# A decoder's cross attentions: heads weighed two chunks at a time, five PSUM banks for scores, queries from unpadded weights

## The chip, the cores and the metric

The kernel runs on one core of a Trainium2 chip. The metric is the device time of one execution in microseconds (us); lower is better. The chip's engines each run their own queue in order: TensorE (PE; its weight loads are listed as PEld), VectorE (DVE), ScalarE (ACT), GpSimd (POOL) and SyncE (SP, which issues DMAs).

## The reference, cut to what matters

The reference is a decoder of four layers over x (8 batches, 112 tokens, 256 features), each layer with a self attention, a cross attention to a context of 8 x 375 x 128, and an FFN. Three of the four cross attentions (layers 1, 2 and 3) go through one helper. With the layer norm in front, layer 1's is

```python
qh = (q @ Wq + bq).reshape(B, LQ, HEADS, D_K).transpose(0, 2, 1, 3)
kh = (k @ Wk + bk).reshape(B, LKV, HEADS, D_K).transpose(0, 2, 1, 3)
vh = (v @ Wv + bv).reshape(B, LKV, HEADS, D_K).transpose(0, 2, 1, 3)
attn = jax.nn.softmax(jnp.einsum('bhqd,bhkd->bhqk', qh, kh) * scale, axis=-1)
out = jnp.einsum('bhqk,bhkd->bhqd', attn, vh)
return concat @ Wo + bo
```

There are 16 heads. Layers 1 and 3 have 16 features a head (the code calls this case `dense`), layer 2 has 32. Layer 3 has no biases.

## The kernel before, in words

`cross` (L1260 to L1447) is that helper; `l1_xattn`, `a2_attend` and `l3_xattn` call it. It takes one batch of 112 tokens after the other, and the 16 heads of a batch in four **chunks** c of four heads j. One chunk of one batch is a **step**; there are 32 in each of the three attentions. What a step consists of:

- `score` (L1326): four matmuls, one a head, each on its own 32 rows of the array, into four PSUM banks `sc` of 112 x 375. TensorE runs an fp32 matmul as two instructions, so the trace has eight.
- `exponent` (L1333): for each head a DVE maximum over the scores (L1338) and an ACT exponential (L1342; in layer 2 L1344, which also sums) into `xe`.
- `turn` (L1347): three transposes of a head's `xe` into a bank `tr`, of which there are two in turn, and the copy `xeT` out of it: by DVE for heads 0 and 2 (L1359), by ACT for heads 1 and 3 (L1357).
- `attend` (L1362): the values times the exponentials, 12 matmuls (24 instructions) on 32 columns of the array each, into one quarter of the bank `av`. After the fourth chunk ACT copies the whole bank to `xoT` (L1377).

Beside these there is work for the neighbouring batches: `key` (L1291, evacuated by ACT) and `value` (L1301, evacuated by DVE) for the next batch; `summed` (L1379: eight tiny matmuls that gather the softmax's denominators, a DVE reciprocal, a POOL copy), `divide` (L1391: four transposes into a `tr` bank, a DVE product) and `result` (L1402: the output projection and the sum into x) for the batch before; and `query` (L1313) for the second half of the tokens. Keys, values, queries, denominators and results all use the one bank `mm`.

The eight PSUM banks are thus: `mm` 1, `av` 1, `tr` 2, `sc` 4.

In layers 1 and 3 a head has 16 features, but a row tile of the array has 32. Keys are kept packed, two heads in 32 rows (`nk` = 2 chunks of 128 rows). `_halves` (L81) therefore spreads the query weights over 512 columns, with zeros where the other head of a pair lies, so that a score over 32 rows sees one head. A half's queries are then four products of 128 columns instead of two.

The order is written out by hand (L1414 to L1447, `manual_schedule` for PE, DVE and ACT): each of these engines executes its instructions in the order of the calls. For a step that is: turn 0, turn 1, key (or summed or divide), turn 2, the scores of the next step, turn 3, the maxima and exponentials of the next step, value, query, result, attend. What lies outside of that block is placed among it by the framework's scheduler.

Of the kernel before, what the change touches and what calls it, by code (L numbers as in the profile page):

```python
# [46 lines left out]
def _fm(w):  # L47

    k, n = w.shape
    return w.reshape(k // P, P, n).transpose(1, 0, 2).reshape(P, -1)  # L50


def _col(v):

    return v.reshape(-1, P).T
# [22 lines left out]
    return w.reshape(-1, 16, 16)[:, _SLOTS].reshape(w.shape)  # L78


def _halves(w):  # L81

    out = np.zeros((w.shape[0], 4, 4, 2, 16), w.dtype)
    a = w.reshape(-1, 16, 16)[:, _SLOTS].reshape(-1, 4, 4, 16)
    for n in range(4):
        out[:, n, :, n % 2] = a[:, n]
    return out.reshape(-1, 512)

_SHIFT = np.tile(np.arange(32) == 16, 16).astype(np.float32)
# [33 lines left out]
def _weights(inp):  # L125
    def g(layer):
# [46 lines left out]
            ("l1a_bo", _row(a("bo"))),  # L173
        ],
        [
            ("l1x_wq", _fm(_halves(xa("Wq")))),
            ("l1x_wk", xa("Wk")),
            ("l1x_wv", _slots(xa("Wv"))),
            ("l1x_bv", _row(_slots(xa("bv")[None])[0])),
# [10 lines left out]
    for j in range(2):  # L190
# [1 line left out]
    v1 = [  # L192
        ("l1a_bq", _col(_spread(a("bq")[None])[0])),
        ("l1a_bk", _col(_spread(a("bk")[None])[0] + _SHIFT)),
        ("l1x_bq", _col(_halves(xa("bq")[None])[0])),
        ("l1x_bk", _col(xa("bk"))),
    ]

# [40 lines left out]
    for pf in ("a1", "a2"):  # L239
        for n in ("lnx_g", "lnx_b", "lny_g", "lny_b", "ln3_g", "ln3_b", "li2_b"):  # L240
# [10 lines left out]
    ]  # L251
    last = [
        [
            ("l3x_wq", _fm(_halves(xa("Wq").T))),
            ("l3x_wk", wkv[:, :D]),
            ("l3x_wv", _slots(wkv[:, D:])),
        ],
# [6 lines left out]
        ("l3f_s_in", np.broadcast_to(f("s_in")[None, :], (P, 1))),  # L264
        ("l3f_s_in_down", np.broadcast_to(f("s_in_down")[None, :], (P, 1))),
    ]
    return (blobs, ternary, last), own, ints, raw, v0 + v1 + v2 + v3


# [110 lines left out]
class _Kernel:  # L380
# [879 lines left out]
    def cross(self, name, cT, qsrc, wq, wk, wv, wo, hd, scale, finish, ctx, bq=None, bk=None, bv=None):  # L1260
# [16 lines left out]
        work = ctx.enter_context(tc.tile_pool(name=f"{name}_w", bufs=2))  # L1277
        ps1 = ctx.enter_context(tc.tile_pool(name=f"ps1_{name}", bufs=1, space=PSUM))
        ps = ctx.enter_context(tc.tile_pool(name=f"ps_{name}", bufs=2, space=PSUM))
        ps4 = ctx.enter_context(tc.tile_pool(name=f"ps4_{name}", bufs=4, space=PSUM))  # L1280

        values = [self.t(acts, [P, NCH, 16, 32], f"xv{i}") for i in range(2)]
        dense = hd == 16
# [7 lines left out]
        def key(b, c):  # L1291
            if c == 0:
                keys[b] = self.t(work, [P, nk, CTX], "xkT")
            pm = self.t(ps1, [P, 512], "mm")[:, :CTX]
            self.mm(pm, [(wk[:, c * P : (c + 1) * P], cT[:, b * CTX : (b + 1) * CTX])])
            if bk is None:
                nc.scalar.copy(keys[b][:, c, :], pm)
            else:
                nc.scalar.activation(keys[b][:, c, :], pm, AF.Identity, bias=self.v(bk, c))

        def value(b, i):  # L1301
            pm = self.t(ps1, [P, 512], "mm")[:CH, : 16 * hd]
            at = b * CTX + i * CH
            self.mm(pm, [(cT[:, at : at + CH], wv)])
            src, dst = pm.rearrange("p (h d) -> p h d", h=16), values[b % 2][:CH, i, :, :hd]
            if bv is None:
                (nc.vector.tensor_copy if b else nc.scalar.copy)(dst, src)
            else:
                nc.vector.tensor_tensor(dst, src, bv[:CH].rearrange("p (h d) -> p h d", h=16), ALU.add)
# [15 lines left out]

        def score(b, c):  # L1326
            toks = slice(b * S, (b + 1) * S)
            es[b, c] = [self.t(ps4, [P, 512], "sc")[:S, :CTX] for _ in range(4)]
# [4 lines left out]
        def exponent(b, c):  # L1333
            if c == 0 and not dense:
                sums[b] = self.t(self.small, [P, 16], "xsu")[:S]
            for j, sc in enumerate(es[b, c]):
                nm = self.t(self.small, [P, 1], f"xnm{j}")[:S]
                nc.vector.tensor_reduce(nm, sc, AX.X, ALU.max, negate=True)  # L1338
                e = self.t(work, [P, CTX], f"xe{j}")[:S]
                at = 4 * c + j  # L1340
                if dense:
                    nc.scalar.activation(e, sc, AF.Exp, bias=nm)  # L1342
                else:
                    nc.scalar.activation(e, sc, AF.Exp, bias=nm, accum_out=sums[b][:, at : at + 1])  # L1344
                es[b, c][j] = e

        def turn(b, c, j):  # L1347
            tp = self.t(ps, [P, 512], "tr")
            e = es[b, c][j]
            for i in range(NCH):  # L1350
                nc.tensor.transpose(  # L1351
                    tp[:CH, i * S : (i + 1) * S], e[:, i * CH : (i + 1) * CH], self.ident[:S, :S]
                )
            eT = self.t(work, [P, NCH, S], f"xeT{j}")[:CH]
            src = tp[:CH, : NCH * S].rearrange("p (c s) -> p c s", c=NCH)
            if j % 2:
                nc.scalar.copy(eT, src)  # L1357
            else:
                nc.vector.tensor_copy(eT, src)  # L1359
            eTs[b, c, j] = eT  # L1360

        def attend(b, c):  # L1362
            if c == 0:
                avs[b] = self.t(ps1, [P, 512], "av")
            for i in range(NCH):
                for j in range(4):
                    nc.tensor.matmul(  # L1367
                        avs[b][32 * j : 32 * j + 32, c * S : (c + 1) * S],
                        values[b % 2][:CH, i, 4 * c + j, :],
                        eTs[b, c, j][:, i, :],  # L1370
                        start=i == 0,
                        stop=i == NCH - 1,
                        skip_group_check=True,
                    )
            if c == 3:
# [15 lines left out]
        def divide(b):  # L1391
            tp = self.t(ps, [P, 512], "tr")
            for c in range(4):
                nc.tensor.transpose(
                    tp[:, c * S : (c + 1) * S],
                    sums[b][:, 4 * c : 4 * c + 4, :].rearrange("p h d -> p (h d)"),
                    self.ident[:S, :S],
                )
            oT = oTs[b]
            nc.vector.tensor_tensor(oT, tp[:, : 4 * S].rearrange("p (c s) -> p c s", c=4), oT, ALU.mult)  # L1400

        def result(b):  # L1402
            finish(b, self.project(ps1, b, [oTs[b][:, c, :] for c in range(4)], wo))
# [3 lines left out]
        for i in range(NCH):  # L1407
            value(0, i)
        qsrc(ps, 0)
        for c in range(4):  # L1410
            query(0, c)
        qsrc(ps, 1)
        steps = [(b, c) for b in range(NB) for c in range(4)]
        with tc.manual_schedule(engines={ET.PE, ET.DVE, ET.Activation}):  # L1414
            score(0, 0)
            exponent(0, 0)
            for n, (b, c) in enumerate(steps):
                turn(b, c, 0)
                turn(b, c, 1)

                if not dense or c % 2 == 0:
                    if b + 1 < NB:
                        key(b + 1, c * nk // 4)
                elif b > 0:
                    (summed, divide)[c // 2](b - 1)
                turn(b, c, 2)
                if n + 1 < len(steps):
                    score(*steps[n + 1])
                turn(b, c, 3)
                if n + 1 < len(steps):  # L1430
                    exponent(*steps[n + 1])
                if c < 3 and b + 1 < NB:
                    value(b + 1, c)
                if c == 3 and b < 2:
                    query(1, 2 * b)
                    query(1, 2 * b + 1)
                if not dense and b > 0 and c == 1:
                    divide(b - 1)
                if b > 0 and c == 3:
                    result(b - 1)  # L1440
                attend(b, c)
# [1237 lines left out]
```

## Time and profile before

| | us |
|---|---|
| median of three runs | 2160.9 (2160.12 to 2161.86) |
| the profiled execution, its own time | 2162.92 |
| span of that execution, first to last instruction | 2161.1 |
| PE busy in the span | 1930.8 (89%) |
| DVE busy | 1388.4 (64%) |
| ACT busy | 867.8 (40%) |
| mean granted TensorE clock | 0.948 |
| transposes of layer 1's cross attention, first and last start | 727.6 and 889.7 |
| the same in layer 2 | 1389.1 and 1556.8 |
| the same in layer 3 | 1880.8 and 2041.4 |

Times in the trace count from the span's start. A line of the timeline gives start, duration, engine, line of the kernel, operation, output and inputs by the program's names, shape, how many instructions were merged into the line, and in brackets how long the engine was idle before it and who released it. A merged line's duration runs to the end of its last instruction; matmuls are pipelined, so the next group starts before that. The three attentions take some 490 us of the span together.

### The profile page before, as it was taken

To read this page: it belongs to the slowest core of one execution; us is meant where nothing else is said; L and a number is where in the kernel's file an instruction comes from. 1 tells how busy PE (TensorE), PEld (TensorE's weight loads), DVE (VectorE), ACT (ScalarE), POOL (GpSimd) and SP (SyncE) were. 2 spreads that over 40 slices of the span, in tenths; PEclk is the share of its full clock that TensorE was granted. 3 is DMA by queue.
4 is the path that set the end of the run, shared out by engine and by line. 5 is a ranking of instruction groups with operands and counts; after the bars stand their busy time and mean duration, and the time that the engine had idled before them with its cause. 6 is when DMAs were issued, how large, how long until landed. Compare 5 with 4: busy or idle time off the path is not lost. (4 is left out here: it accounts for less than half of the span.)

```text
span 2161.1 us, 45441 instructions
## 1 busy us (share of the span) xinstructions
PE 1930.8 (89%) x17912; PEld 1242.8 (58%) x17912; DVE 1388.4 (64%) x3907; ACT 867.8 (40%) x2420; POOL 279.0 (13%) x480
## 2 busy tenths in 40 slices
PE   7999999898898899889899989899999997899844
PEld 3555544465666566546566555556567885566623
DVE  5666666576555577553566675567624866667688
ACT  2444444562212356453033223466525322356532
POOL 1111111001301100000001342100103420100000
PEclk9999999999899999999999999999999997999956
DMA  5000001103000000224101010000021310000000
GB/s 208 3 3 3 3 22 39 33 21 107 1 1 16 21 2 2 79 77 148 40 1 59 1 47 3 1 2 2 1 80 70 99 38 26 1 2 2 2 1 17
DMA packets 11486, 69.20 MB, mean 32 GB/s; under 512 B 1290, under 2 KB 3082, under 8 KB 4874
## 3 DMA queue, kind: packets, MB, share of 16 engines
q1 hardware_dynamic: 9684, 54.69, 7.1%
q0 software_dynamic: 1584, 11.54, 1.5%
q8 instruction: 145, 2.38, 0.4%
q14 instruction: 73, 0.60, 0.1%
HBM read 65.30 MB, written 0.92 MB: 31 GB/s over the span
## 5 line engine op out<-in xcount | busy, mean ns | idle before, releaser
L727 PE MATMUL g<-w,hT 128*32 128x256 f32 x3552 | 236.8, 384 | 1.8 <-DVE hT L757 1.5
L1338 DVE TENSOR_REDUCE xnm<-sc 112x1 f32<-112x375 f32 x384 | 184.6, 541 | 40.5 <-PE sc L444 39.8
L1351 PEld LDWEIGHTS tr<-cst,xe 112*125 112x125 f32 x1152 | 151.5, 188 | 94.6 <-issue 38.1
L1351 PE MATMUL tr<-cst,xe 112*125 112x112 f32 x1152 | 192.9, 289 | 6.8 <-DVE xeT L1359 4.2
L727 PEld LDWEIGHTS g<-w,hT 128*32 128x32 f32 x3552 | 93.2, 109 | 121.9 <-DVE hT L757 82.9
L1357 ACT COPY xeT<-tr 125x336 f32<-125x336 f32 x192 | 85.0, 443 | 158.3 <-PE tr L1351 158.3
L444 PE MATMUL mm<-xnT,w 128*128 128x448 f32 x316 | 136.9, 575 | 9.7 <-DVE qT L1320 2.9
L1359 DVE COPY xeT<-tr 125x336 f32<-125x336 f32 x192 | 97.3, 507 | 68.6 <-PE tr L1351 61.8
L690 PE MATMUL g<-xw,cst 128*32 128x256 f32 x1792 | 137.9, 379 | 0.0
L1342 ACT ACTIVATE xe<-sc,xnm 112x375 f32<-112x375 f32 x256 | 126.4, 582 | 7.3 <-DVE xnm L1338 7.3
L753 ACT ACTIVATE th<-cell 128x64 f32<-128x64 f32 x224 | 57.5, 257 | 144.3 <-DVE cell L749 141.8
L444 PE MATMUL mm<-w,hT 128*112 128x256 f32 x448 | 101.6, 387 | 0.0
L740 ACT ACTIVATE sg<-g 128x192 f32<-128x192 f32 x224 | 73.9, 330 | 67.7 <-PE g L727 45.8
L444 PEld LDWEIGHTS mm<-xnT,w 128*128 128x128 f32 x316 | 60.2, 201 | 68.4 <-issue 44.6
L444 PE MATMUL mm<-hThi,w 128*128 128x448 f32 x256 | 94.3, 368 | 0.0
L444 PE MATMUL mm<-hTlo,w 128*128 128x448 f32 x256 | 93.9, 367 | 0.0
L576 POOL TENSOR_TENSOR hTlo<-xnT,hThi 128x448 fp32r<-128x448 f32 x60 | 72.2, 1211 | 161.7 <-ACT hThi L574 88.0
L758 POOL COPY hs<-hT 128x16 f32<-128x16 f32 x224 | 51.5, 230 | 319.0 <-DVE hT L757 319.0
L444 PEld LDWEIGHTS mm<-w,hT 128*112 128x112 f32 x448 | 80.6, 181 | 19.9 <-issue 2.3
L755 DVE TENSOR_TENSOR h<-sg,th 128x64 f32<-128x64 f32 x224 | 50.5, 225 | 63.9 <-ACT th L753 63.8
L444 PE MATMUL sc<-xkT,qT 32*112 32x375 f32 x768 | 89.8, 519 | 0.0
L1367 PE MATMUL av<-xeT,xv 125*32 125x112 f32 x2304 | 86.4, 266 | 2.1 <-ACT xeT L1357 2.1
(485 smaller groups left out, 3961.2 us busy)
## 6 DMA issues: line engine op xcount, KB each, us to landing
w<-in_w SPq DMA_DIRECT2D x22, 1024.0 KB, 5.0
t<-in_wt SPq DMA_DIRECT2D x11, 1024.0 KB, 4.9
w<-in_wt POOLq DMA_DIRECT2D x11, 1024.0 KB, 5.3
raw<-in_wq SPq DMA_DIRECT2D x3, 1024.0 KB, 4.9
cx<-in_ctx SPq DMA_DIRECT2D x2, 1500.0 KB
wi<-in_wint SPq DMA_DIRECT2D x3, 768.0 KB, 5.6
w<-in_w SPq DMA_DIRECT2D x2, 896.0 KB, 10.4
w<-in_w SPq DMA_DIRECT2D x2, 768.0 KB, 4.3
```

Of the source, the lines that this page charges most:

```text
L444: self.nc.tensor.matmul(out, lhsT, rhs, start=i == 0, stop=i == len(pairs) - 1)
L576: nc.gpsimd.tensor_tensor(dst[1], src, dst[0].bitcast(F32), ALU.subtract)
L690: nc.tensor.matmul(g[32 * j : 32 * j + 32, :], pick[:, t % 16, :], xw[:, l, t // 16, 256 * j : 256 * j + 256], start=True, stop=t == 0, sk ...
L727: nc.tensor.matmul(g[32 * j : 32 * j + 32, :], hT[l][:, c, :], whh[l][:, c, 256 * j : 256 * j + 256], start=False, stop=c == 1, skip_group ...
L740: nc.scalar.activation(sg[:, :192], g[:, :192], AF.Sigmoid)
L753: nc.scalar.activation(th, cell[l], AF.Tanh)
L1338: nc.vector.tensor_reduce(nm, sc, AX.X, ALU.max, negate=True)
L1342: nc.scalar.activation(e, sc, AF.Exp, bias=nm)
L1351: nc.tensor.transpose(tp[:CH, i * S : (i + 1) * S], e[:, i * CH : (i + 1) * CH], self.ident[:S, :S])
L1357: nc.scalar.copy(eT, src)
L1359: nc.vector.tensor_copy(eT, src)
L1367: nc.tensor.matmul(avs[b][32 * j : 32 * j + 32, c * S : (c + 1) * S], values[b % 2][:CH, i, 4 * c + j, :], eTs[b, c, j][:, i, :], start=i ...
```

## The change

- **Queries.** `_halves` goes; the query weights are unpadded (256 columns). A dense `query` makes one product of 128 columns and evacuates it twice, multiplied by a vector `turn0` or `turn1` that is 0.25 on the even or the odd blocks of 16 rows and zero on the others. With a bias (layer 1) both evacuations are DVE's; without (layer 3) one is DVE's and one ACT's. A dense half has two calls of `query` instead of four.
- **Banks.** `sc` has five banks; `av` goes, and `attend` writes into the bank `mm`.
- **Two chunks together.** `attend(b, c - 1)` runs once in two steps, after the odd chunk, with 48 instructions; the new `attended` copies its half of `xoT` with DVE, so twice a batch.
- **Order.** An even step runs as before without attend. An odd step runs: turn 0, key (or summed or divide), turns 1, 2 and 3, value, query, result, the next scores, attend, the first three maxima and exponentials of the next step, the copy `attended`, the fourth maximum and exponential. Layer 2's queries of the second half are spread over the odd steps, one in each.

```diff
-        ps4 = ctx.enter_context(tc.tile_pool(name=f"ps4_{name}", bufs=4, space=PSUM))
+        ps5 = ctx.enter_context(tc.tile_pool(name=f"ps5_{name}", bufs=5, space=PSUM))
...
-            if bq is None and half == 0:
+            if dense:
+                for p in range(2):
+                    out, even = qT[:, 2 * c + p, cols], self.v(f"turn{p}")
+                    if bq is not None:
+                        nc.vector.tensor_scalar(out, pm, self.v(bq, c), even, ALU.add, ALU.mult)
+                    elif p:
+                        nc.scalar.activation(out, pm, AF.Copy, scale=even)
+                    else:
+                        nc.vector.tensor_scalar(out, pm, even, None, ALU.mult)
+            elif bq is None and half == 0:
...
         def attend(b, c):
+
+            avs[b] = self.t(ps1, [P, 512], "mm")[:, : 2 * S]
+            for h in range(2):
+                for i in range(NCH):
+                    for j in range(4):
+                        nc.tensor.matmul(
+                            avs[b][32 * j : 32 * j + 32, h * S : (h + 1) * S],
+                            values[b % 2][:CH, i, 4 * (c + h) + j, :],
+                            eTs[b, c + h, j][:, i, :],
+                            start=i == 0,
+                            stop=i == NCH - 1,
+                            skip_group_check=True,
+                        )
+
+        def attended(b, c):
             if c == 0:
...
                 oTs[b] = self.t(work, [P, 4, S], "xoT")
-                nc.scalar.copy(oTs[b], avs.pop(b)[:, : 4 * S].rearrange("p (c s) -> p c s", c=4))
+            nc.vector.tensor_copy(oTs[b][:, c : c + 2, :], avs.pop(b).rearrange("p (c s) -> p c s", c=2))
...
-        for c in range(4):
+        for c in range(nk):
             query(0, c)
...
+                def first():
+                    if not dense or c % 2 == 0:
+                        if b + 1 < NB:
+                            key(b + 1, c * nk // 4)
+                    elif b > 0:
+                        (summed, divide)[c // 2](b - 1)
+
+                def second():
+                    if c < 3 and b + 1 < NB:
+                        value(b + 1, c)
+                    if dense and c == 3 and b < 2:
+                        query(1, b)
+                    elif not dense and c % 2 and b < 2:
+                        query(1, 2 * b + c // 2)
+                    if not dense and b > 0 and c == 1:
+                        divide(b - 1)
+                    if b > 0 and c == 3:
+                        result(b - 1)
+
                 turn(b, c, 0)
...
+                if c % 2 == 0:
+                    turn(b, c, 1)
+                    first()
+                    turn(b, c, 2)
                     score(*steps[n + 1])
...
+                    turn(b, c, 3)
                     exponent(*steps[n + 1])
...
+                    second()
+                    continue
+                first()
+                for j in range(1, 4):
+                    turn(b, c, j)
+                second()
+                for s in following:
+                    score(*s)
+                attend(b, c - 1)
+                for s in following:
+                    exponent(*s, range(3))
+                attended(b, c - 1)
+                for s in following:
+                    exponent(*s, range(3, 4))
```

More of the change, by code (lines that the diff above doesn't have):

```diff
@@ L78, in _slots @@
     return w.reshape(-1, 16, 16)[:, _SLOTS].reshape(w.shape)
[L81 to L87, printed above, removed]
+_EVEN = [(np.arange(P) // 16 % 2 == p).astype(np.float32)[:, None] for p in range(2)]
 _SHIFT = np.tile(np.arange(32) == 16, 16).astype(np.float32)
@@ L175, in _weights @@
         [
-            ("l1x_wq", _fm(_halves(xa("Wq")))),
+            ("l1x_wq", _fm(xa("Wq"))),
             ("l1x_wk", xa("Wk")),
@@ L194, in _weights @@
         ("l1a_bk", _col(_spread(a("bk")[None])[0] + _SHIFT)),
-        ("l1x_bq", _col(_halves(xa("bq")[None])[0])),
+        ("l1x_bq", _col(xa("bq"))),
         ("l1x_bk", _col(xa("bk"))),
@@ L253, in _weights @@
         [
-            ("l3x_wq", _fm(_halves(xa("Wq").T))),
+            ("l3x_wq", _fm(xa("Wq").T)),
             ("l3x_wk", wkv[:, :D]),
@@ L266, in _weights @@
     ]
+    v3 += [(f"turn{p}", np.float32(0.25) * _EVEN[p]) for p in range(2)]
     return (blobs, ternary, last), own, ints, raw, v0 + v1 + v2 + v3
@@ L1327, in score @@
             toks = slice(b * S, (b + 1) * S)
-            es[b, c] = [self.t(ps4, [P, 512], "sc")[:S, :CTX] for _ in range(4)]
+            es[b, c] = [self.t(ps5, [P, 512], "sc")[:S, :CTX] for _ in range(4)]
             for j, sc in enumerate(es[b, c]):
@@ L1331, in score, with exponent @@
                 self.mm(sc, [(qT[r, c, toks], keys[b][r, c * nk // 4, :])])
-        def exponent(b, c):
-            if c == 0 and not dense:
+        def exponent(b, c, js=range(4)):
+            if c == 0 and js[0] == 0 and not dense:
                 sums[b] = self.t(self.small, [P, 16], "xsu")[:S]
-            for j, sc in enumerate(es[b, c]):
+            for j in js:
+                sc = es[b, c][j]
                 nm = self.t(self.small, [P, 1], f"xnm{j}")[:S]
@@ L1362, in attend @@
         def attend(b, c):
-            if c == 0:
[L1364 to L1375, printed above, removed]
+            avs[b] = self.t(ps1, [P, 512], "mm")[:, : 2 * S]
[11 more added lines that the diff above has]
+        def attended(b, c):
+            if c == 0:
                 oTs[b] = self.t(work, [P, 4, S], "xoT")
-                nc.scalar.copy(oTs[b], avs.pop(b)[:, : 4 * S].rearrange("p (c s) -> p c s", c=4))
+            nc.vector.tensor_copy(oTs[b][:, c : c + 2, :], avs.pop(b).rearrange("p (c s) -> p c s", c=2))
         def summed(b):
@@ L1417, in cross @@
             for n, (b, c) in enumerate(steps):
-                turn(b, c, 0)
[L1419 to L1427, printed above, removed]
+                following = steps[n + 1 : n + 2]
+                def first():
[4 more added lines that the diff above has]
+                        (summed, divide)[c // 2](b - 1)
@@ L1428, in cross @@
+                if c % 2 == 0:
+                    turn(b, c, 1)
+                    first()
+                    turn(b, c, 2)
                     score(*steps[n + 1])
-                turn(b, c, 3)
-                if n + 1 < len(steps):
+                    turn(b, c, 3)
                     exponent(*steps[n + 1])
[L1432 to L1441, printed above, removed]
+                    second()
[9 more added lines that the diff above has]
+                    exponent(*s, range(3))
```

## Prediction

> **What bounds the kernel now.** I read the page first, then busy time by stretches over settled batches of the three attentions, then the timeline of single steps, then what the scores and transposes waited for, last the granted clock. The page says that PE is busy most of the time; the stretches, one batch each, say by how much here (columns: stretch, its length, then PE, PEld, DVE, ACT, POOL busy with instruction counts, the granted clock):
>
> ```profile
> 812.50:832.00 19.50, 19.14 (x214) 13.35 (x206) 14.52 (x33) 12.38 (x28) 0.61 (x1) 1.00 0.01 2
> 1457.80:1478.40 20.60, 20.39 (x210) 13.02 (x202) 15.10 (x33) 14.55 (x46) 1.28 (x2) 1.00 0.01 2
> ```
>
> PE 98%, DVE 75%, ACT 63 to 71%: PE is the bound, and nothing is hidden that costs PE time. One step of layer 1 in the timeline shows how the order achieves this:
>
> ```profile
> 780.08 0.90 PE L444 MATMUL sc<-xkT,qT 32*112 32x375 f32 x8
> ...
> 780.91 0.58 PE L1351 MATMUL tr<-cst,xe 112*125 112x112 f32 x3
> 781.07 1.91 DVE L1338 TENSOR_REDUCE xnm<-sc 112x1 f32<-112x375 f32 x4 [0.37 <-PE sc L444]
> ...
> 781.33 0.61 PE L444 MATMUL mm<-w,ctxT 128*125 128x256 f32 x2
> 781.58 0.44 ACT L1357 COPY xeT<-tr 125x336 f32<-125x336 f32 x1 [2.00 <-PE tr L1351]
> ...
> 781.86 0.97 PE L1367 MATMUL av<-xeT,xv 125*32 125x112 f32 x24
> 781.91 1.97 ACT L1342 ACTIVATE xe<-sc,xnm 112x375 f32<-112x375 f32 x4
> ...
> 782.76 0.91 PE L1351 MATMUL tr<-cst,xe 112*125 112x112 f32 x6
> 782.89 0.42 DVE L1309 TENSOR_TENSOR xv<-mm,w 125x256 f32<-125x256 f32 x1
> 783.38 0.51 DVE L1359 COPY xeT<-tr 125x336 f32<-125x336 f32 x1
> 783.51 0.81 PE L444 MATMUL mm<-ctxT,w 128*128 128x375 f32 x2
> ...
> 784.15 0.48 PE L1351 MATMUL tr<-cst,xe 112*125 112x112 f32 x3
> ```
>
> Count from the scores at 780.08. The first maximum starts at 0.99, the first exponential at 1.83 (ACT copies `xeT` of head 3 first) and ends at 2.41 (one takes 0.58 by the page). The next transposes start at 2.68: the exponential is ready 0.27 early, because turn 3 (0.33), the value (0.46) and attend (0.90 to the next transpose) stand between. The next scores come at 4.48. By first transposes, the four steps of a settled batch last 4.48, 4.64, 4.48 and 5.88 us in layers 1 and 3 (19.49), and 4.72, 5.11, 5.16, 5.58 in layer 2 (20.57).
>
> Prices, from the same rows: three transposes 0.33; key 0.65 on PE; scores 0.83; layer 1's value 0.46, layer 2's 0.88; `summed` 0.72; `divide` 0.41; `result` 1.83; maxima 0.456 apart, exponentials 0.46 (layer 2: 0.55); from a transpose's end to its copy 0.04 (DVE) or 0.09 (ACT); from a copy's end to PE 0.05 to 0.15.
>
> **The fifth bank.** Before the scores PE was never released by an exponential: nothing waits for a bank of `sc`, so it buys nothing as such. The Trainium skill (Perfetto Trace Analysis, Optimization Strategy) says that a gap which repeats on the engine that should be saturated can mean too little PSUM for the next tile. No such gap stands before these scores, so by the row the rule gives nothing here.
>
> **An even step after.** Count from the scores S that feed it. Attend with 48 instructions follows them: 0.83 + 1.27 (24 issue in 0.52 where nothing waits, layer 2's row of 0.78 less one's 0.26; twice that, 0.04 between, and 0.19 to the next transpose), so PE is free at 2.10. Exponential 0, with ACT free, runs 1.57 to 2.15; turn 0 starts at 2.24. `attended` (0.40, below the 0.51 of 336 columns) waits behind maximum 2, 2.37 to 2.77; maximum 3 starts at 2.70; the copy of head 0 ends at 3.67; so turn 2 starts at 3.81 and the next scores, 0.41 later as at 784.15, at 4.22. Key and turn 1 fit between.
>
> Now the new wait. From these scores PE has turn 3 and the value, to 1.70, then turn 0 of the odd step, which needs the exponential that ends at 2.41: it starts at 2.50, a **wait of 0.8** (layer 2: 0.4, its value is longer). Attend, which covered this, is gone. Behind it in PE's queue stands everything.
>
> **An odd step, layers 1 and 3.** *First pair* (key, value; summed, value): turn 0 ends at 2.83. `summed` needs the bank `mm`, which DVE empties after its four maxima, 2.82 to 3.23: starts 3.37, **waits 0.54**, ends 4.09. Turn 1 at 4.09, turn 2 at 4.42; turn 3 needs turn 1's bank, whose ACT copy runs 4.67 to 5.11: starts 5.26, **waits 0.51**. Value to 6.05, scores at 6.13. The pair lasts 4.22 + 6.13 = 10.35; before 4.48 + 4.64 = 9.12: **+1.23**. *Second pair*: turn 0, divide to 3.24; turn 1 waits for the copy of head 0 (behind the value's on DVE, to 3.69), 3.84; turn 2 for divide's product (to 4.27), 4.42; turn 3 for turn 1's copy, 5.00; result 5.33 to 7.16, scores 7.24. 11.46 against 10.36: **+1.10**. Here divide occupies one of the two `tr` banks, and the three transposes in a row have nothing between them.
>
> **Layer 2.** The exponential wait is 0.4, but the odd step's key waits for the value's copy (0.68 after the maxima, to 3.43), 3.57; turn 3 waits for ACT, which copies the key before head 1, 5.42; value and divide to 7.05, scores 7.13: 4.22 + 7.13 = 11.35 against 9.83, **+1.5**. Second pair, with the result in place of value and divide: 4.22 + 7.66 = 11.88 against 10.74, **+1.1**, and 0.2 for the reciprocal that now stands before a transpose copy: +2.85 a batch.
>
> **Queries.** A query is four instructions, 1.55, and PE then waits for its copy out of `mm`: 2.55 each in the rows (718.35, 720.90, 723.45, 726.00). Before the loop, four become two, with two copies of 0.68 in DVE's queue (layer 1) or one on each engine (layer 3): -3.0 and -3.6 up to the first transpose. In the loop (steps that lasted 7.87 and 10.98 in layer 1) two become one; attend then waits for its second copy. Walked as above: -1.3 and -0.8 in layer 1, -1.8 and -1.3 in layer 3. Together **-12**. Layer 2 keeps its queries, each waiting once more for `mm`: +1.
>
> **Sum.** Layers 1 and 3: five settled batches x 2.33, +1.2 for the second batch's first pair, +0.5 for the ends, is 13.4 each, 26.8; less 12 is +15. Layer 2: 5 x 2.85, +2.9 and +1.9 for the two batches with queries, +0.8 for the last, +1: +21. The norm statistics that the framework places on DVE behind `result` now stand before a maximum that PE waits for: 24 x 0.2, half absorbed, +2.
>
> **The clock.** One old step shows what idleness costs:
>
> ```profile
> 837.73 0.95 PE L444 MATMUL mm<-cst,xoT 128*112 128x4 f32 x8 [0.23 <-DVE xv L1309]
> 838.89 0.55 PE L1351 MATMUL tr<-cst,xe 112*125 112x112 f32 x3 [0.20 <-DVE xeT L1359]
> ```
> ```profile
> 830.00:850.00 20.00, 19.20 (x194) 13.42 (x192) 15.00 (x44) 12.26 (x27) 0.61 (x1) 0.91 0.00 1
> ```
>
> Two waits beside the tiny matmuls of `summed`, and right after them the clock is at half for some 3.5 us (0.91 over 20 us is 1.8 lost, at half speed 3.6); these two steps lasted 6.39 and 4.92 in place of 4.64 and 4.48, 2.2 more. In my first pair of layers 1 and 3 the stretch from 1.7 to 5.1 holds 1.1 us of transposes in 3.4, beside the tiny matmuls. Such stretches come 14 times (7 batches in 2 layers). None of them is as sure to slow the clock as a long idle time; I take half, at 1.5 each (3.5 us at half speed is 1.75, a part of it PE would have waited): 10, less the 2.2 of the old one: +8.
>
> The Trainium skill (TensorE: Matmul & The Clock Gate, Part 1: The HAM clock gate) lets the clock depend on activity in freely running windows of about 3.4 us; the row's 3.5 agrees, and it would make chance decide which stretches are hit. The same skill (TensorEngine Tiling (Array Packing), Key Properties) says that a change of tiling mode drains TensorE. That speaks for this change: a pair changes mode five times in place of eight. The rows show at most 0.19 for one (attend to transposes), so at most 0.57 a pair; 2 x 0.90 - 1.27 = 0.53 of that is in the walk already, and by the rule at its largest the sum would be 48 x 0.04, 2 us, lower.
>
> 15 + 21 + 2 + 8 = **+46**: 2162.9 + 46 = 2208.9 for an execution like the profiled one; the median stands 2.0 below it: **2207**.
>
> **Rivals.**
> - *The clock decides* (15%): all 48 odd steps have a low stretch, and if some 27 lose 1.7 us each, 46 in place of 8: 2245. For it: the row above. Against: result and layer 2's key fill most of the others.
> - *The odd step's waits are covered* (8%): if the copies on DVE and ACT come soon enough, only the wait for the exponential is new. First pair 10.35 - 1.05 = 9.30, second 11.46 - 1.10 = 10.36, layer 2 about +0.2 a pair; the pairs give +6 in all, the queries -12: 2155, **faster**. It decides once a value's copy is done before turn 0; against it: it stands behind four maxima in DVE's queue, at 782.89 too.
> - *PE alone counts* (4%): matmuls of the first pair sum to 7.9, some 8.3 with gaps, 0.8 less than now; 48 x -0.8 - 12: 2111. Against: the waits above are in the order of each queue.
> - *Gains and waits cancel* (5%): per pair about 0.3.
>
> The forecast's mechanism holds 68%. **Range:** at its low end each walked pair is 0.4 shorter (latencies of 0.05 instead of 0.15 at three or four places) and the clock stays: 2207 - 19 - 8 = 2180; I go to 2174 for the queries, known to some 6 us. At the high end three times the clock's share and 12 for strays: 2207 + 16 + 12 = 2235. Within 0.2% (4.3 us) is about what a measurement here can't tell from no change: 5%; faster 12%; slower 83%.
>
> **What would show it.** Right: first transposes of a settled batch 21 to 22.5 us apart in layers 1 and 3, 23 to 24 in layer 2; PE busy there about 85%; transposes (L1351) idle some 50 us in all, released by ACT `xe`, and more by `xeT`; `summed` and layer 2's key waiting for DVE `xv`; fewer instructions of `mm<-xnT,w`; several intervals of half clock within the attentions. Wrong: steps of 19 us or less, or an even step whose transposes do not wait after the value.

## The result, and the profile after

The changed kernel takes **2243.4 us** (median of 4 runs, 2241.3 to 2247.6) against 2161.4 (4 runs, 2160.1 to 2164.6): 1.038 times as long, 95% interval 1.0359 to 1.0400. That is +82 where +46 was forecast, and above the range (2235). The profiled execution took 2241.3; its span is 2239.6, its mean granted clock 0.931 (before 2161.1 and 0.948).

Net, the whole loss lies in the three attentions; outside of them gains and losses cancel. From their first to their last transpose they take 189.0, 193.3 and 186.2 us (before 162.1, 167.7, 160.6): +78.1 of the span's +78.5. The settled batches, by stretches, in the changed kernel (columns as in the prediction):

```profile
797.10:820.50 23.40, 21.22 (x206) 14.20 (x206) 14.79 (x35) 12.15 (x27) 0.61 (x1) 0.93 0.00 1
820.50:842.40 21.90, 19.62 (x206) 13.22 (x206) 14.72 (x35) 12.21 (x27) 0.61 (x1) 1.00 0.01 2
...
1469.40:1492.70 23.30, 21.27 (x203) 13.34 (x203) 15.28 (x35) 13.98 (x45) 1.34 (x2) 1.00 0.01 2
```

The first two are neighbouring batches of layer 1 with the same instructions on every engine. One keeps the full clock and lasts 21.9, as the walk said (10.35 + 11.46 = 21.81). The other shows a mean clock of 0.93 and lasts 1.5 longer. The third, layer 2, lasts 23.3 (walk: 23.23). PE is busy 90 to 91% of such a batch, not 98%.

Its page answers to the groups of before (the first line below is the kernel before): the transposes have gone from 6.8 us of idle time ahead of them to 47.4, most of it ended by ACT's exponentials (21.7 in layers 1 and 3, 7.0 in layer 2), and 32 instructions of the query product are gone (316 before).

```profile
L1351 PE MATMUL tr<-cst,xe 112*125 112x112 f32 x1152 | 192.9, 289 | 6.8 <-DVE xeT L1359 4.2
```
```profile
L1355 PE MATMUL tr<-cst,xe 112*125 112x112 f32 x1152 | 212.1, 305 | 47.4 <-ACT xe L1346 21.7
...
L438 PE MATMUL mm<-xnT,w 128*128 128x448 f32 x284 | 124.2, 582 | 5.7 <-DVE xnT L431 2.0
```

One first pair of layer 1 in the timeline of the changed kernel, from the scores that feed it to the next pair:

```profile
799.18 0.90 PE L438 MATMUL sc<-xkT,qT 32*112 32x375 f32 x8
...
800.16 1.91 DVE L1342 TENSOR_REDUCE xnm<-sc 112x1 f32<-112x375 f32 x4 [0.37 <-PE sc L438]
...
800.42 0.61 PE L438 MATMUL mm<-w,ctxT 128*125 128x256 f32 x2
...
801.01 1.97 ACT L1346 ACTIVATE xe<-sc,xnm 112x375 f32<-112x375 f32 x4
...
801.64 0.58 PE L1355 MATMUL tr<-cst,xe 112*125 112x112 f32 x3 [0.61 <-ACT xe L1346]
801.99 0.41 DVE L1303 TENSOR_TENSOR xv<-mm,w 125x256 f32<-125x256 f32 x1
...
802.46 0.95 PE L438 MATMUL mm<-cst,xoT 128*112 128x4 f32 x8 [0.23 <-DVE xv L1303]
...
803.26 0.89 PE L1355 MATMUL tr<-cst,xe 112*125 112x112 f32 x6
...
804.40 0.58 PE L1355 MATMUL tr<-cst,xe 112*125 112x112 f32 x3 [0.26 <-ACT xeT L1361]
...
804.82 0.61 PE L438 MATMUL mm<-w,ctxT 128*125 128x256 f32 x2
...
805.36 1.52 PE L438 MATMUL sc<-xkT,qT 32*112 32x375 f32 x8
...
806.81 2.35 PE L1372 MATMUL mm<-xeT,xv 125*32 125x112 f32 x48
```

Counted from 799.18, turn 0 starts at 2.46 (walk 2.50), `summed` at 3.28 (3.37), turn 1 at 4.08 (4.09), turn 3 at 5.22 (5.26), the next scores at 6.18 (6.13). The waits are where the walk has them. What it did not price stands in the last two lines: these scores take 1.52 in place of 0.90, attend 2.35 (1.36 in an undisturbed pair). The same stretch in slices of 2 us:

```profile
799.20:801.20 2.00, 1.83 (x14) 0.88 (x13) 1.55 (x4) 0.93 (x3) 0.00 (x0) 1.00 0.00 0
801.20:803.20 2.00, 1.33 (x11) 1.15 (x11) 1.62 (x4) 1.78 (x4) 0.00 (x0) 1.00 0.00 0
803.20:805.20 2.00, 1.74 (x14) 1.39 (x13) 0.77 (x2) 0.56 (x2) 0.61 (x1) 1.00 0.00 0
805.20:807.20 2.00, 2.00 (x20) 0.77 (x22) 0.67 (x2) 0.31 (x1) 0.00 (x0) 0.57 0.00 0
807.20:809.20 2.00, 2.00 (x49) 1.79 (x38) 1.21 (x3) 1.50 (x3) 0.00 (x0) 0.57 0.04 8
```

PE idles about a quarter of 801 to 805, and then runs at half clock for (0.43 + 0.43) x 2 / 0.5 = 3.4 us, right when scores and attend are due and nothing makes it wait.

### The profile page after: what moved, and what is told of

It reads as the page before. It is cut to its first block, busy times and chain, and to the rows that moved or that the text cites. A ratio compares the mean times of both kernels' runs of the same rounds, so it can differ in the third digit from the quotient of the medians.

```text
span 2239.6 us, 45374 instructions
## 1 busy us (share of the span) xinstructions
PE 1962.4 (88%) x17880; PEld 1258.6 (56%) x17880; DVE 1399.5 (62%) x3955; ACT 860.5 (38%) x2396; POOL 280.1 (13%) x480
## 5 line engine op out<-in xcount | busy, mean ns | idle before, releaser
L1355 PE MATMUL tr<-cst,xe 112*125 112x112 f32 x1152 | 212.1, 305 | 47.4 <-ACT xe L1346 21.7
L1355 PEld LDWEIGHTS tr<-cst,xe 112*125 112x125 f32 x1152 | 161.0, 195 | 152.0 <-ACT xe L1346 53.8
L1346 ACT ACTIVATE xe<-sc,xnm 112x375 f32<-112x375 f32 x256 | 129.9, 577 | 95.8 <-DVE xnm L1342 95.5
L438 PE MATMUL mm<-xnT,w 128*128 128x448 f32 x284 | 124.2, 582 | 5.7 <-DVE xnT L431 2.0
L438 PE MATMUL sc<-xkT,qT 32*112 32x375 f32 x768 | 100.0, 580 | 1.5 <-DVE qT L1319 0.9
L1348 ACT ACTIVATE xe<-sc,xnm 112x375 f32<-112x375 f32 x128 | 71.8, 575 | 47.9 <-DVE xnm L1342 47.9
L438 PEld LDWEIGHTS mm<-xnT,w 128*128 128x128 f32 x284 | 55.3, 204 | 57.1 <-issue 42.1
```

What stands on the lines that cost most here:

```text
L438: self.nc.tensor.matmul(out, lhsT, rhs, start=i == 0, stop=i == len(pairs) - 1)
L1355: nc.tensor.transpose(tp[:CH, i * S : (i + 1) * S], e[:, i * CH : (i + 1) * CH], self.ident[:S, :S])
```

## The theories

**Mine, after the result:** the walked waits are right, and the extra loss is the clock: the waits of the first pairs in layers 1 and 3 let it fall far oftener than "half of 14, 1.5 each". **The rival:** the clock is a by-product; the extra loss is unpriced waits (the queries, the fifth bank, another order on DVE and ACT), and an execution with the full clock would be nearly as long.

## The experiments

Steps below are from first transposes to first transposes in each run's trace: c0 to c3 are the four steps of a batch.

**1. Queries alone**, in the kernel before (the new `query` and its weights are those of the change above).

```diff
...
-                    query(1, 2 * b)
-                    query(1, 2 * b + 1)
+                    query(1, b * nk // 2)
+                    if not dense:
+                        query(1, 2 * b + 1)
```

> The kernel before with the unpadded queries alone; order and banks as before. If the queries give what the prediction said (two products of 1.55 us and their waits saved before each loop and two within it), 2161 - 12 = 2149 us, with the first transposes of layers 1 and 3 some 3 to 4 us after less of a prologue. If the doubled evacuations cost as much as the products saved, 2161.

2153.6 (2144.9 to 2158.1), ratio 0.995 (0.9929 to 0.9971). The part gains, and this is the fastest version of this study. In the trace the attentions of layers 1 and 3 are 3.6 and 2.9 shorter, the stretches up to their first transposes 2.1 and 2.3: 10.9, close to the 12. But the stretch between the attentions of layers 1 and 2, which the edit does not touch, is 5.6 longer, with 61.4 us at half clock in place of 47.8 (mean clock 0.94 and 0.95). So where the half clock falls can shift by some microseconds when work ahead of it is moved.

**2. Order alone**: the changed kernel with the queries padded again.

```diff
...
-        for c in range(nk):
+        for c in range(4):
             query(0, c)
...
-                        query(1, b)
+                        query(1, 2 * b)
+                        query(1, 2 * b + 1)
```

> The changed kernel with the padded queries of before: order and banks alone. If the two parts add up, 2243 + 12 = 2255 us. If the new order makes room for the queries, or the clock takes most of the loss, nearer to 2243.

2247.6 (2245.7 to 2253.9), ratio 1.0399 (1.0373 to 1.0424): the order costs it all. In the changed kernel the queries are worth some 4 us, not the 9 of experiment 1, and the executions of the two kernels overlap. In the profiled ones, up to the first transposes they save 8.4 (4.4 and 4.0), and 2.8 come back in the two attentions, whose half clock falls otherwise (41.0 and 30.7 us of it in place of 20.5 and 23.9).

**3. Four banks for scores** in the changed kernel.

```diff
-        ps5 = ctx.enter_context(tc.tile_pool(name=f"ps5_{name}", bufs=5, space=PSUM))
+        ps5 = ctx.enter_context(tc.tile_pool(name=f"ps5_{name}", bufs=4, space=PSUM))
```

> The changed kernel with four score banks in place of five. Walked by the rows, the fourth exponential of a step ends 0.4 us before the next scores need its bank, so 2243 us as it was. If the fifth bank carries the new order, each even step waits: 48 x 0.3 or more, 2258 and up.

2243.8 (2241.9 to 2250.1), ratio 1.0381 (1.0356 to 1.0407): the same as with five. The fifth bank buys nothing, as no wait for a bank of scores in the profile had foretold. It is free for other uses below.

**4. Unread products in the waits.** Four banks for scores; the fifth takes products that nothing reads, placed where PE waits. The order of all else stays.

```diff
...
+        def fill(n):
+            self.mm(spare[:, :n], [(self.ident, self.ctxT[:, :n])])
...
                     second()
+                    fill(320 if dense else 160)
                     continue
+                if dense and c == 1:
+                    fill(256)
+                elif not dense:
+                    fill(320)
                 first()
-                for j in range(1, 4):
+                for j in range(1, 3):
                     turn(b, c, j)
+                fill(224 if c == 1 or not dense else 128)
+                turn(b, c, 3)
```

> Four score banks, and the freed bank takes matmuls that nobody reads, put where PE waits in the new order (0.2 to 0.6 us each: ahead of the odd step's first transposes, ahead of summed or layer 2's key, ahead of turn 3). They add work and remove no wait. If the half clock makes up the loss beyond the walked waits (18 slow intervals in the three attentions of the changed kernel against one before), most of these intervals go and the time falls by 20 to 30 us, to about 2215. If the loss is waits alone, 2243 or more.

2215.1 (2212.2 to 2219.5), ratio 1.0246 (1.0225 to 1.0268), clock 0.949 in the profiled execution. **More work, 28 us less.** The waits are still there, but PE does not stand in them. The same two waits of the first pair in its timeline:

```profile
793.60 0.70 PE L438 MATMUL spare<-ctxT,cst 128*128 128x320 f32 x2
...
794.38 0.58 PE L1356 MATMUL tr<-cst,xe 112*125 112x112 f32 x3
...
794.80 0.61 PE L438 MATMUL spare<-ctxT,cst 128*128 128x256 f32 x2
...
795.25 0.90 PE L438 MATMUL mm<-cst,xoT 128*112 128x4 f32 x8
...
798.10 0.90 PE L438 MATMUL sc<-xkT,qT 32*112 32x375 f32 x8
```

The next scores come 6.19 after those at 791.91, as in the changed kernel, but take 0.90; the next pair starts on time. Settled steps are 4.52, 5.97, 4.45, 6.95 (layer 2: 4.62, 6.77, 4.59, 7.31), the length of the changed kernel's where its clock stays up. Of its 18 intervals of half clock within the attentions 3 are left, one in each sixth batch. The rival falls: 28 us of the loss are the clock.

**5. Unread products in the first pairs of layers 1 and 3 alone.**

```diff
+                    if dense and c == 0:
+                        fill(320)
                     continue
...
+                if dense and c == 1:
+                    fill(256)
                 first()
...
+                if dense and c == 1:
+                    fill(224)
+                turn(b, c, 3)
```

> The changed kernel with four banks of scores, and unread matmuls only in the waits of the first pair of each batch in layers 1 and 3. If the slow clock in those pairs is what lengthens their odd step from 5.97 to 7.4 to 8.5 us, that step goes back to 5.97 in nearly all of the 14 pairs and the time falls by 16 to 20 us, to about 2223 to 2228. If the second pairs or the sixth batch set the slow clock off, most of the long steps stay and the time is above 2235.

2227.0 (2221.9 to 2228.2), ratio 1.0297 (1.0266 to 1.0328): 16 us less than the changed kernel. The odd step of the first pair is back at 5.97 or 5.98 (6.19 once, 5.83 in the sixth batches, 5.49 in the last). In the changed kernel it took 7.0 to 8.5 in 11 of 14 pairs: these 11 are called hit below. Two second pairs now take 8.63 in place of 6.95: the fall is not removed for good, only less often met.

**6. Value ahead of the last maxima** in the even step, so that `summed` finds its bank free.

```diff
-                    exponent(*steps[n + 1])
+                    exponent(*steps[n + 1], range(2))
                     second()
+                    exponent(*steps[n + 1], range(2, 4))
                     continue
```

> The changed kernel; in an even step DVE empties the value's bank after two maxima instead of four. By the walk summed then starts with no wait: the first pair of layers 1 and 3 loses 0.9 us (10.45 to about 9.6), the second none; layer 2 gains 0.4 at its key and loses 0.6 at turn 3 because the fourth exponential is later: about +0.2 a pair. Waits: 14 x -0.9 + 3 = -10 us; with fewer stretches of little work some slow intervals go too: 2220 to 2230. If the value's copy behind four maxima is not what summed waits for: 2243.

2225.9 (2224.1 to 2239.8), ratio 1.0305 (1.0265 to 1.0344). Undisturbed first pairs: odd step 5.49 in place of 5.97; layer 2's odd steps are 0.25 longer (7.02, 7.55), since their last exponentials come later. 14 x 0.48 less 14 x 0.25 is 3 of the 17 gained; the rest I put down to the clock, which rose to 0.940 (7 of the 14 first pairs are hit in its profile, in place of 11). The waits gave half of what was expected, 0.48 in place of 0.9 a pair; the total came out in the expected range by the clock.

**7. Turn 3 behind value and result** in the odd step.

```diff
                 first()
-                for j in range(1, 4):
+                for j in range(1, 3):
                     turn(b, c, j)
                 second()
+                turn(b, c, 3)
```

> The changed kernel; in an odd step turn 3 stands behind the value, query and result, so that PE has work while turn 1's bank is copied out. By the walk first pairs lose 0.46, second 0.25, layer 2's 0.4 each: 14 x 0.7 + 15 x 0.4 = -16 us, and some slow intervals: 2215 to 2225. If the two transpose banks are not the limit there: 2243.

2215.9 (2214.5 to 2222.1), ratio 1.0247 (1.0221 to 1.0272). Odd steps 5.53 and 6.63 (0.44 and 0.32 less), layer 2 6.42 and 6.95 (0.35 each). That is 14 x 0.76 + 14 x 0.35 = 15.5; the rest of the 27 I put down to fewer falls of the clock in the first pairs (7 of 14 hit). A turn that only waits for a copy belongs behind work that waits for nothing.

**8. A bank of its own for the value product**, the one that the scores do not need.

```diff
...
-            pm = self.t(ps1, [P, 512], "mm")[:CH, : 16 * hd]
+            pm = self.t(psv, [P, 512], "vm")[:CH, : 16 * hd]
```

> The changed kernel with four banks of scores; the bank left over takes the value products, which no longer share the bank mm with keys, denominators and attend. If the waits of summed and of layer 2's key are for that one bank, as the walk has it, the first pair's odd step in layers 1 and 3 falls from 5.97 to about 5.5 us where nothing disturbs it, layer 2's odd steps from 6.77 and 7.31 to about 6.1 and 6.7, some 15 us in all, and the shorter waits slow the clock less: 2215 to 2228 us. If these steps are set by VectorE's queue itself, in which the value's copy stands behind four maxima whatever its bank, the steps stay and the time is 2240 to 2246.

2213.9 (2210.9 to 2217.4), ratio 1.0225 (1.0208 to 1.0242). In layers 1 and 3 the wait of `summed` is gone (5.97 to 5.49), so it was the bank (14 x 0.48 and 14 x 0.08 are 8 of the 29 gained; 6 of the 14 first pairs are hit in place of 11, and the rest was not followed). In layer 2 the walk was half right. The key comes early now, 0.42 behind turn 0, but the step falls only to 6.69, and the wait stands further back:

```profile
1492.05 0.58 PE L1356 MATMUL tr<-cst,xe 112*125 112x112 f32 x3 [0.28 <-ACT xe L1349]
...
1492.47 0.81 PE L438 MATMUL mm<-yT,w 128*128 128x375 f32 x2
...
1493.54 0.49 ACT L1292 COPY xkT<-mm 128x375 f32<-128x375 f32 x1
1493.89 0.48 ACT L1362 COPY xeT<-tr 125x336 f32<-125x336 f32 x1
...
1494.73 0.55 PE L1356 MATMUL tr<-cst,xe 112*125 112x112 f32 x3 [0.69 <-DVE xeT L1364]
```

Turn 3 (1494.73) now waits 0.69. ACT's copy of head 1, which empties its bank, stands behind the key's copy and ends at 1494.37; the profile names DVE's copy of head 2, to 1494.58, as the last releaser, and why that one counts is not settled. Two waits lay one behind the other, and taking the first away uncovered the second.

**9. The copy `attended` behind all four maxima.** The sixth batch of each attention has a first step of 8.0 to 8.8 in place of some 4.5. The timeline of the changed kernel in layer 2 shows why:

```profile
1538.90 0.52 DVE L1342 TENSOR_REDUCE xnm<-sc 112x1 f32<-112x375 f32 x1
...
1539.33 0.16 DVE L449 TENSOR_SCALAR va<-mv 112x4 f32<-112x4 f32 x1
1539.53 0.17 DVE L452 TENSOR_SCALAR r<-va 112x4 int32<-112x4 int32 x1
...
1541.11 0.16 DVE L463 SCALAR_TENSOR_TENSOR rs<-rw,rp 112x4 f32<-112x4 f32 x1
1541.31 0.41 DVE L484 TENSOR_SCALAR xn<-xo,mv,rs 112x256 f32<-112x256 f32 x1
1541.64 0.38 DVE L1384 COPY xoT<-mm 128x224 f32<-128x224 f32 x1
...
1542.08 0.96 PE L438 MATMUL mm<-yT,w 128*128 128x375 f32 x2 [1.69 <-DVE xoT L1384]
```

After the fourth result the next stage's norm can begin for half of the tokens, and the framework puts its chain of small dependent DVE operations, 2.3 us, into the gap between the third maximum and `attended`. The key behind it on PE waits 1.7 for the bank. In the kernel before, the chain cost an odd step at most 1.75 (6.39 for 4.64 in layer 1, where the clock fell in that step; 1.13 and 0.83 in layers 2 and 3), and there attend had a bank of its own and a copy on ACT, so that the key did not wait for that copy.

```diff
                 for s in following:
-                    exponent(*s, range(3))
+                    exponent(*s)
                 attended(b, c - 1)
-                for s in following:
-                    exponent(*s, range(3, 4))
```

> The changed kernel; attended's copy stands behind all four maxima. Then DVE no longer has an idle slot while it waits for attend, into which the framework put the next stage's norm (a chain of small operations, in the sixth batch of each attention, where a step lasts 8.2 to 8.8 in place of 4.5). If that placement costs, these steps fall to about 5.5 and the time by 8 to 11 us, to 2233; the other steps stay, since the copies that gate turn 2 keep their place. If the sixth batch is slow for another reason: 2243.

2245.1 (2242.2 to 2249.3), ratio 1.0368 (1.0347 to 1.0390): a miss in total. The sixth batches' first steps did fall to 6.0, but nearly every even step pays: 5.06 in place of 4.62 for layer 2's c0, where turn 2 now comes 2.0 behind turn 0 in place of 1.6, some 0.16 in layers 1 and 3. The profile names ACT's copy of head 1 as the releaser there; why the turn waits for that one is not settled.

**10. The same in the sixth batch alone.**

```diff
+                early = 4 if b == 4 and c == 3 else 3
                 attend(b, c - 1)
                 for s in following:
-                    exponent(*s, range(3))
+                    exponent(*s, range(early))
                 attended(b, c - 1)
                 for s in following:
-                    exponent(*s, range(3, 4))
+                    if early < 4:
+                        exponent(*s, range(3, 4))
```

> The changed kernel with the copy of the attended heads behind the four maxima in one step per layer only, the first of the sixth batch. If the next stage's norm chain, put into VectorE's gap ahead of that copy, is what lengthens that step to 8.0 to 8.8 us, the step falls to about 6 us in each layer with no price elsewhere: 2234 to 2237 us. If the chain's work is only moved to another wait, the time stays at 2240 to 2246.

2242.7 (2237.9 to 2245.4), ratio 1.0365 (1.0331 to 1.0400), no gain that can be told. The first steps are 7.59, 6.01 and 6.01, but the next ones 9.12, 7.52 and 9.34 in place of 7.01, 7.10 and 7.01. What is left of the chain now stands among the next four maxima. Only in layer 2 does something stay (15.9 for both steps became 13.5). **In layers 1 and 3 the chain was moved, not hidden**: my expectation that it has no price elsewhere was wrong. In these next steps `summed`, which did not wait there in the changed kernel, waits 0.65 and 0.89 for the value's copy, and the clock is at half for 6.8 us; how much of the 9.12 and 9.34 is the chain and how much the clock is not separated.

**11. Experiments 6, 7 and 9 together.**

```diff
-                    exponent(*steps[n + 1])
+                    exponent(*steps[n + 1], range(2))
                     second()
+                    exponent(*steps[n + 1], range(2, 4))
...
-                for j in range(1, 4):
+                for j in range(1, 3):
                     turn(b, c, j)
                 second()
+                turn(b, c, 3)
...
-                    exponent(*s, range(3))
+                    exponent(*s)
                 attended(b, c - 1)
```

> The three edits together: value early, turn 3 later, copy last. Walked: first pairs of layers 1 and 3 10.48 to 9.4, second 11.45 to 11.2, layer 2 about -0.2 a pair: -22 us of waits; -8 for the norms; the half clock mostly gone, -20: 2190 to 2195. If order and clock are one loss, as the walk with a clock that follows from it says, the gains add like this; the wait for the exponential, 0.8 us a pair, stays, and so it stays above 2161.

2202.5 (2201.4 to 2203.8), ratio 1.0174 (1.0154 to 1.0195), clock 0.942. Half of the loss is taken back by order alone, less than the expected 2190 to 2195. The settled pairs of layers 1 and 3 are 9.65 and 11.24, close to the walk, but layer 2's first pairs are 11.74, 0.35 longer than in the changed kernel where 0.2 less was walked; the rest of the miss was not followed.

**12. Experiments 6 and 7 with unread products** in the waits that stay.

```diff
...
-                    exponent(*steps[n + 1])
+                    exponent(*steps[n + 1], range(2))
                     second()
+                    exponent(*steps[n + 1], range(2, 4))
+                    fill(320 if dense else 160)
                     continue
+                if not dense:
+                    fill(160)
                 first()
+                if dense and c == 3:
+                    fill(256)
-                for j in range(1, 4):
+                for j in range(1, 3):
                     turn(b, c, j)
                 second()
+                turn(b, c, 3)
```

> The value move brought forward and the late turn of the odd step moved back, with four banks of scores and unread matmuls in the waits that stay. If the clock is the part of the loss that the forecast mis-sized, the granted clock is about 0.945 to 0.95, the settled pairs of layers 1 and 3 take about 9.8 to 10.2 us and 11.1, and the time is 2185 to 2200 us. If the slow stretches only follow from the length of a wait and not from TensorE standing idle in it, the clock stays near 0.935 and the time at 2200 to 2210, no better than the three moves without the unread matmuls (2202). Either way above the kernel before (2161), because the wait for the exponential stays.

2191.3 (2188.8 to 2193.4), ratio 1.0131 (1.0100 to 1.0163), clock 0.947: 11 less than experiment 11, which also differs by the late copy of experiment 9. The settled pairs are 9.49 and 11.08 in layers 1 and 3, 11.27 and 11.78 in layer 2 (before 9.12, 10.36, 9.83, 10.74). Even with these repairs each pair stays longer than the same two steps were before. What is left I put down to the waits that attend covered before; the value's own bank was not tried together with them.

## Why the prediction was wrong

Sign and mechanism were right; the size of the clock's term was not. Experiment 4 splits the loss: its profiled span, 2210.4, is what the order costs with the clock nearly held, and the 29.2 from there to 2239.6 is the clock. Three things blur the split: the falls that are left in the sixth batches count with the norm work; the unread products lengthen a few steps (0.27 in the first batches of layers 1 and 3, 0.5 in layer 2's sixth); and some 6.7 of the queries' row is what comes off up to the first transposes, which was 4.4 in experiment 1. Step by step, with the forecast's terms and what the traces of experiment 4 and of the changed kernel show for them (us):

| term | forecast | measured |
|---|---|---|
| settled pairs of layers 1 and 3 (five batches each) | +23.3 | +24.5 |
| their second batch's first pair, and the ends | +3.4 | +4.8 |
| their first batch's first pair | not priced | +2.2 |
| layer 2 | +21 | +20.4 |
| norm work on DVE (the sixth batch) | +2 | +8.0 |
| queries | -12 | -10.7 |
| stretches between the attentions, apart from the queries | 0 | +0.5 |
| clock | +8 | +29.2 |
| sum | +46 | +78.9 (the spans differ by 78.5) |

- **The walk** was right: 10.48 and 11.46 measured for the pairs of layers 1 and 3 (10.35 and 11.46), 11.39 and 11.90 for layer 2's (11.35 and 11.88). The three named waits are in the timeline at 0.61, 0.23 and 0.26 of idle PE; the walked 0.8, 0.54 and 0.51 count from the last issue, the profile from the modelled end of the matmul before. One detail of layer 2's reason was incomplete: two waits in a row, not one (experiment 8).
- **The fifth bank** buys nothing: right (experiment 3).
- **The step that failed is the clock**: "Such stretches come 14 times ... I take half, at 1.5 each". In the changed kernel 11 of the 14 first pairs are hit, and their odd steps lose 17.4 in all against experiment 4, 1.6 each; 5.1 more fall into other steps (second pairs, last batches), and 6.7 outside of the attentions, where a fall that begins at an attention's end, or one that merely comes at another moment, lengthens the next stage. Count and place were wrong more than price. The traces show what decides the count. In every run all changes of the granted clock lie on one grid of 3.41 us. In the five runs with these waits (the changed kernel, experiments 2, 3, 9 and 10) the clock fell in all 44 first pairs of layers 1 and 3 whose `summed` starts 0.7 to 3.2 us behind a line of that grid, and in 6 of the other 26: 50 of 70, not half (the bounds were read off these runs). Where it starts 1.7 us or more behind the line, two intervals of half clock reach the step in place of one: 8.4 to 9.3 us in place of 7.0 to 7.5 (last batches aside). The number 2245 of the rival "the clock decides" is close by luck: it had some 27 of 48 odd steps hit at 1.7, and the walked queries and strays as in the forecast.
- **The strays** failed too: 0.2 for each norm statistic, but not the whole chain once per attention, in a gap that the new order opened ahead of a copy that PE waits for. +8 in place of +2.
- **The range** had +16 for the clock and +12 for the strays at its high end. They came out at +21 and +6, and some 6 more came from terms that the range took as sure (settled pairs, first batches, ends, queries). The last 4 of the 36 by which the median missed 2207 are scatter: the profiled execution stood 2.0 above its median before and 2.0 below it after.
- **What would show it** came in the main: batches of 21.9 where the clock stayed up (23.4 where it fell, above the 22.5 given) and of 23.3 in layer 2, idle time ahead of the transposes 47.4 (about 50), fewer query products. PE's share is above the 85%, in the batch at full clock too (19.62 of 21.90), so half-clocked matmuls are not the reason; as with the waits, the profile counts a matmul as busy to its modelled end.

The Trainium skill (TensorE: Matmul & The Clock Gate, Why this matters for your kernels) asks for no idle gap of PE above some 3 us if the clock is to stay up. The rows differ: the longest wait in the pair above is 0.61 us, and the clock fell. The same page (Part 1: The HAM clock gate) says that the windows run freely; the grid of 3.41 us above, and two batches with the same instructions and different clocks, agree with that. PE's busy time alone does not say which grid interval is too idle: in the pair above PE was busy 2.93 of the 3.42 us from 802.08 on, and the clock fell; one batch later it was busy 2.57 of the 3.42 us from 822.56 on, and the clock stayed. The first held `summed` and transposes, the second began with scores. How little activity is too little, and of which kind, these runs do not settle.

## What to carry to other kernels

When an order is walked by hand on a PE that is almost always busy, a wait can cost twice, as here: its own length, and the chance that several short ones within 3 to 4 us halve the clock for the next 3.4 us or more. Count every stretch that has them (here 7 in 10 were hit), and look for cover first: the work that waits for nothing goes where PE would stand. A copy that PE waits for should not sit behind a gap on its engine: here the framework's scheduler filled that gap with another stage's work.

## What the runs showed of the hardware

- Work that nothing reads made the kernel 28 us faster (256 more PE instructions in the span: 18136 against 17880). It was put where PE waited, lengthened no settled step, and kept the clock (0.949 against 0.931 in the profiled executions).
- Of the 18 falls of the clock in the attentions 14 last 3.41 us, as the one in the kernel before (3.5 by the prediction's row), three 6.83 and one 17.07, all multiples of 3.41. A fall comes at the next line of the grid, after the idle stretch, so it hits whatever is next: in the pair shown, scores and attend.
- The share of the time at half clock does not order the kernels: experiment 8 has 0.933 and 2213.9, experiment 6 has 0.940 and 2225.9. Only the steps tell what a fall costs.
